# Normed rows of x on GpSimd, a longer warm-up and other first DMA durations in a planned two-layer kernel

## The chip, the cores and the metric

The kernel runs on one core of one Trainium2 chip. A core has five engines with instruction queues of their own: TensorE (PE, matrix products; its weight loads are shown apart as PEld), VectorE (DVE), ScalarE (ACT), GpSimd (POOL) and SyncE (SP, which here issues every DMA). The metric is device time in microseconds, the median of several runs. Lower is better.

## The reference

The input is x, 2 sequences of 1024 rows with 256 features, a context of 154 rows per sequence, and one condition vector per sequence. Two layers follow each other.

```
# layer 0: cross attention with adaptive layer norm
h   = (x - mean) / sqrt(var + eps)                # per row of x, and of the context
xq  = (1 + scale_q) * h + bias_q                  # scale, bias from silu(cond) @ Wss_q + bss_q
xkv = the same on the context rows, with Wss_kv
q, k, v = xq @ Wq + bq, xkv @ Wkv + bkv           # 16 heads of 16
x   = x + softmax(q k^T / 4) v @ Wp + bp
# layer 1: mixture of three experts
nx  = layernorm(x) * gamma + beta
evidence = softmax((nx Wq1)(ctx Wk1)^T / 16) (ctx Wv1)
combined = [nx, evidence, cond]                   # 768 features
probs = softmax(combined @ router_W + router_b)
h_e = silu(combined @ e_w1[e] + e_b1[e])          # 512 wide, three experts
routed = sum_e probs[e] * (h_e @ e_w2[e] + e_b2[e])
g   = sigmoid(silu(combined @ gate_w1 + gate_b1) @ gate_w2 + gate_b2)
out = x + g * (routed @ out_w + out_b)
```

So each row of x is normed twice, once ahead of each layer: its mean is subtracted and the result multiplied by its reciprocal deviation.

## The kernel before, in words

The 2048 rows of x are 16 tiles of 128 rows. Layer 0 (`layer0`) runs 128 steps, 8 for each tile: scores on PE into PSUM, the row maximum on DVE (`mx`, L929), the exponential on ScalarE (L952), a split in two halves of fp16 (`ehl`, L636 on ScalarE and L643 on DVE), a transposing DMA into `et`, and on PE the product with the values (`vm`). `half_done` and `tile_done` divide by the sum (`rc`, `an`, `ao`, L868 to L870), project and add to x (`xa`, L890). The second sequence's rows are in `xb`.

A second stream (`fill`, and after it `dense`) prepares layer 1's weights (`nx`, `evh`, `evl`, `vs`, `vsr`, `ab`) and then computes layer 1 by blocks of one or two pairs of tiles: first the expert layer (`zh`, `zl` and `wh`, `wl`, `wr` against `nx` and `vsr`), tanh on ScalarE (`th`, L1390), a product on DVE (L1393), a split on POOL (`hh` at L638, `hl` at L643), and then the second matrices (`w2oh`, `w2ol`). Numbers are split in a high and a low fp32r part, and three products of parts replace one fp32 product.

The norm of the rows needs four pieces. `stats` computes mean and variance of one tile on DVE (L670, L671). `rstd` turns variances into reciprocal deviations by three Newton steps on tiny tiles (L652 to L665): the first four operations' integer part is on DVE, and the rest is on DVE where `soon` is set, else on POOL. Then one `tensor_scalar` per tile subtracts and multiplies and writes `xn`, a buffer of which two exist: ahead of layer 0 in `front_norm` (L803), ahead of layer 1 in `a` of `front1` (L1021). PE transposes `xn` (L619), and ScalarE applies scale and bias (`full`, L826 and L1028). `moments(i0, i1)` computes the statistics of tiles i0 to i1 ahead of layer 0; its first call also takes the three tiles of context rows (`ctn`) and computes all six deviations together. The context rows are normed on DVE at L1115.

The prologue (`start`) computes scale and bias from the condition vector (`adaptive`, for the context with the weights `wsskv` and for x with `wssq`: 16 small matmuls into PSUM, a copy `ss` on ScalarE, a transpose on PE, and `ada` on DVE), norms and transposes the context, applies scale and bias to it (`xk`, L1124 on ScalarE), and makes keys and values. Meanwhile PE runs `WARM` matmuls on zeros (`warm`), whose results nobody reads, so that it doesn't idle.

The order of all instructions on each engine is not the order of the source. `Plan` builds a graph of all instructions, gives each a duration (`price`), and lists them by rank with a table of durations; `MOVES` is a list of random changes of the ranks that are kept where they shorten the planned total. The resulting order of each engine is then fixed by dependencies (`pin`). A warm-up matmul has the lowest rank: it stands where the plan finds PE without other work. A DMA's planned duration is its bytes divided by a rate. SP issues all DMAs in the planned order: before the change the context rows, the first two tiles of x, `vec` (the small vectors, the condition among them), `wsskv`, `wssq`, the key weights, the query weights, two more tiles of x, the value weights and so on.

Of the kernel before, what the change touches and what calls it, by code (L numbers as in the profile page):

```python
# [16 lines left out]
ALU = mybir.AluOpType  # L17
# [6 lines left out]
NT = 16  # L24
# [3 lines left out]
HK = 160  # L28
EPS = 1e-5
NE = 3  # L30
WARM = 60
RAW = 6
LEAD = 1
BLOCKS = ((0, 1), (1, 1), (2, 2), (4, 2), (6, 2))
NSTEP = 8 * NT
PACE0, PACE1 = 1500.0, 2100.0
MOVES = (1100001, 1100005, 1100019, 1100033, 1100059, 1100068, 1100087, 1100091, 1100170, 1100261, 1100302,
         1100322, 1100329, 1100338, 1100420, 1100424, 1100527, 1100533, 1100618, 1100719, 1100724, 1100868,
         1100955, 1100984, 1100999, 1101051, 1101060, 1101194, 1101201, 1101272, 1101290, 1101335, 1101413,
         1101426, 1101441, 1101487, 1101528, 1101561, 1101574, 1101614, 1101671, 1101704, 1101924, 1102111,  # L40
         1102322, 1102606, 1102710, 1102758, 1102833, 1103118, 1103684, 1104487, 1104919, 1105278, 1105605,
         1105610, 1105611, 1105652, 1105670, 1105798, 1105925, 1106150, 1107392, 1107479, 1107593, 1107732,
         1107777, 1107785)


V_BQ, V_BSSQ, V_BSSKV, V_GAM, V_BET, V_COND, V_BK, V_B2 = 0, 2, 6, 10, 12, 14, 18, 20
# [3 lines left out]
class Later:  # L50


    def __init__(self):
        self.now, self.due = 0, {}
# [50 lines left out]
class Plan:  # L105
# [5 lines left out]
    SBUF = 212800  # L111

    def __init__(self, tc):
        self.tc, self.nc = tc, tc.nc
        self.side, self.tiles, self.names = {}, {}, 0
        self.kept = {}
        self.streams = set()
        self.joint = {}
        self.apart = {}
# [154 lines left out]
    def price(self, node, op):  # L274

        ins, eng = node.ins, node.eng
        aps = [a for a in ins.ins if hasattr(a, "bass_ap")]
        outs = [a for a in ins.outs if hasattr(a, "ap")]
        node.cost = 50.0
        if not outs:  # L280
            return
        n = count(list(outs[0].ap)[1:])
        if eng == "SP":
            b = count(outs[0].ap) * mybir.dt.size(outs[0].dtype)
            turn = "Transpose" in op
            node.cost = b / 311.0 if not turn else b / 160.0
            node.load = 900.0 if not turn and outs[0].dtype == FP16 else 650.0 if turn or (len(outs[0].ap) > 2 and b < 200000) else 475.0
            node.wide = 1470.0 if turn else node.load
            return
        widths = [count(list(a.ap)[1:]) for a in aps]  # L290
        psum = any(self.side.get(self.tiles.get(str(getattr(a.bass_ap.tensor, "name", "")).rpartition("_")[0],
                                                ("",))[0]) == str(PSUM) for a in aps)
        ptr = sum(1 for w in widths[1:] if w == 1 and n > 1)
        wide = [a for a, w in zip(aps, widths) if w > 1 or n == 1]


        flat_ = sum(self.side.get(self.tiles.get(str(getattr(a.bass_ap.tensor, "name", "")).rpartition("_")[0],
                                                 ("",))[0]) != str(PSUM) for a in wide)
        node.port = eng == "Pool" or (eng == "DVE" and op not in ("TensorReduce", "BNStats", "BNStatsAggregate", "Reciprocal")
                                      and not (len(wide) == 1 and psum) and flat_ > (0 if len(wide) == 1 else 1))  # L300
        if eng == "PE":
            m, four = widths[-1], aps[-1].dtype in (F32, F32R)
            passes = 1 if aps[0].dtype != F32 else 2 if ins.is_transpose else 4
            node.cost = max(passes * n / 2.4, 20.0) + 2.5 + (5.9 + 0.0172 * n if aps[0].dtype == F32R else 0.0)
            node.load = (m / 4 if not four else 4 * m if passes == 4 else 2 * m) / 2.4
            node.rows = list(aps[0].ap)[0][1] / P
            if list(outs[0].ap)[0][1] == 32:

                node.cost, node.load = node.cost / 3, node.load / 3
            if ins.name in self.joint:  # L310

                node.rows, node.step, node.cost = 1.0, node.cost, 280.0
        elif eng == "Activation":
            node.cost = 0.833 * n + (50 if psum else 94) + 93 * ptr
        elif eng == "Pool":
            node.cost = (0.83 * n + 36 if op == "Memset" else 2.08 * n + 160 if op == "TensorTensor" else 0.833 * n + 160)
        elif not aps:
            node.cost = 10.0 + 1.04 * n
        else:
            w = max([n] + widths)  # L320
            single = sum(1 for k in widths if k > 1) == 1 and not psum and op != "TensorReduce"
            node.cost = (335.0 if op == "BNStats" else 290.0 if op == "ISA" else 115.0 if op == "Reciprocal" else 75.0 if w < 16
                         else (0.52 if single else 1.04) * w + 65 + 64 * ptr)
# [218 lines left out]
def tile_pixart_cross_moe(  # L542
# [27 lines left out]
    V, S, G, T, Q = nc.vector, nc.scalar, nc.gpsimd, nc.tensor, nc.sync  # L570
# [74 lines left out]
    def rstd(out, var, n, pool, soon=False):  # L645


        E = V if soon else G
        v = tl(pool, [P, n], F32, f"nwv{n}")
        h = tl(pool, [P, n], I32, f"nwh{n}")  # L650
        t = tl(pool, [P, n], F32, f"nwt{n}")
        V.tensor_scalar(v, var, EPS, None, ALU.add)  # L652
        V.tensor_scalar(h, v.bitcast(I32), 1, None, ALU.logical_shift_right)
        V.tensor_scalar(h, h, -1.0, float(0x5F3759DF), ALU.mult, ALU.add)
        E.tensor_scalar(v, v, -0.5, 1.0, ALU.mult, ALU.mult)
        cur = h.bitcast(F32)
        for _ in range(3):
            E.tensor_tensor(t, cur, cur, ALU.mult)
            if soon:
                E.tensor_tensor(t, t, v, ALU.mult)  # L660
                E.scalar_tensor_tensor(out, t, 1.5, cur, ALU.add, ALU.mult)
            else:
                E.tensor_tensor(t, t, v, ALU.mult)
                E.tensor_scalar(t, t, 1.5, 1.0, ALU.add, ALU.mult)
                E.tensor_tensor(out, t, cur, ALU.mult)  # L665
            cur = out

    def stats(mv, src, pool):
        st = tl(pool, [P, 6], F32, "bnst", 2)[: src.shape[0]]
        V.bn_stats(st, src)  # L670
        V.bn_aggr(mv, st)  # L671
# [9 lines left out]
    xres = [xa[:, i] for i in range(NT // 2)]  # L681
    mv0 = tl(per, [P, 20, 2], F32, "mv0")
    rs0 = tl(per, [P, 20], F32, "rs0")
# [36 lines left out]
    CT = (P, P, 52)  # L720
# [65 lines left out]

    def moments(i0, i1):

        k0 = 4 + i0
        if i0 == 0:  # L790
            k0 = 0
            for i, n in enumerate(CT):
                stats(mv0[:n, i], ctn[:n, i], ta)
        for i in range(i0, i1):
            stats(mv0[:, 4 + i], xres[i], l0)
        k = slice(k0, 4 + i1)
        rstd(rs0[:, k], mv0[:, k, 1], 4 + i1 - k0, l0, i0 == 0)

    def front_norm(hb):
        xns = []  # L800
        for i in range(2 * hb, 2 * hb + 2):
            xn = tl(l0, [P, 256], F32, "xn", 2)
            V.tensor_scalar(xn, xres[i], mv0[:, 4 + i, 0:1], rs0[:, 4 + i : 5 + i], ALU.subtract, ALU.mult)  # L803
            xns.append(xn)
        return xns

# [91 lines left out]
    def layer0(later):  # L898
        ao, ets = None, []
        for p in range(NSTEP):  # L900
            ti, j = divmod(p, 8)
            b, q0 = ti // 8, (ti % 2) * P
            if j == 0:
                ao = tl(l0, [P, 256], F32, "ao", 2)
                if ti == 1:
                    moments(4, NT // 2)
                if ti == 6:
                    while len(xres) < NT:
                        yield
                    moments(8, NT)  # L910
                if ti % 2 == 0 and ti + 2 < NT:
                    front(ti // 2 + 1, later)
            if j % 4 == 0:
# [81 lines left out]
    def front1(hb, later):  # L995
# [14 lines left out]
        def a():  # L1010
            if hb == NT // 4:
                ones(1)
            mv = tl(keep["lf"], [P, 2, 2], F32, "mv1", 2)
            rs = tl(keep["lf"], [P, 2], F32, "rs1", 2)
            for i in range(2):
                stats(mv[:, i], xres[t0 + i], keep["lf"])
            rstd(rs, mv[:, :, 1], 2, keep["lf"], hb < 2)
            st["xn"] = []
            for i in range(2):
                xn = tl(l0, [P, 256], F32, "xn", 2)  # L1020
                V.tensor_scalar(xn, xres[t0 + i], mv[:, i, 0:1], rs[:, i : i + 1], ALU.subtract, ALU.mult)  # L1021
                st["xn"].append(xn)

        def t():
# [82 lines left out]

    def start():

        adaptive(1)  # L1110
        adaptive(0)
        moments(0, 2)
        norm, turn, q, stack = front(0, None, first=True)
        for i, n in enumerate(CT):
            V.tensor_scalar(ctn[:n, i], ctn[:n, i], mv0[:n, i, 0:1], rs0[:n, i : i + 1], ALU.subtract, ALU.mult)  # L1115
# [66 lines left out]
        G.tensor_scalar(bph, bpr, 1.0, 1.0, ALU.mult, ALU.mult)  # L1182
        G.tensor_scalar(f(bph), f(bph), mneg, 1.0, ALU.mult, ALU.mult)
        G.tensor_tensor(bp2[0:2], f(bph), bpr, ALU.add)
        moments(2, 4)
        trA.close()


# [399 lines left out]
```

## Time and profile before

| what | value |
|---|---|
| median of 3 runs | 403.0 us (402.08 to 403.06) |
| the profiled execution's own time | 405.18 us |
| its span, first to last instruction | 403.4 us |
| mean granted clock of PE | 0.989 |
| busy, share of the span | PE 96%, PEld 82%, DVE 77%, ACT 56%, POOL 51% |
| DMA | 40.60 MB in packets, 101 GB/s on average |

All durations below come from one profiled execution, which was 2.18 us slower than the median. In the profile, a line such as L615 is often a helper's: all matmuls stand at L615, all transposes at L619, all splits at L636 to L643, and only the names of the tiles tell which is which. Busy time counts overlapping matmuls once. "Granted clock" is the share of full speed at which PE was allowed to run.

### The profile page before, as it was taken

What the parts mean: (1) busy time and instruction counts of PE and PEld (TensorE: products, weight loads), DVE (VectorE), ACT (ScalarE), POOL (GpSimd) and SP (SyncE); (2) the same over time, 40 slices, a digit from 0 to 9 for tenths busy, and PEclk for the clock granted to TensorE, in tenths of its full rate; (3) what the DMA queues carried; (4) which work ended last, traced back from release to release, by engine and by line L of the source; (5) the groups of instructions that cost most, each with busy time, mean ns of one, the idle gap of its engine ahead of it and who ended that gap; (6) DMA issues with size and microseconds to landing.
All of it is one profiled execution on the core that took longest, in us unless ns stands there. A gap on an engine that the chain in (4) does not pass through costs nothing. (4 is left out here: it accounts for less than half of the span.)

```text
span 403.4 us, 8995 instructions
## 1 busy us (share of the span) xinstructions
PE 388.0 (96%) x3206; PEld 331.1 (82%) x3206; DVE 309.3 (77%) x837; ACT 226.2 (56%) x607; POOL 206.4 (51%) x369
## 2 busy tenths in 40 slices
PE   6999999789999999999999999999999999999995
PEld 4787776577799999999879888888788989888884
DVE  7468988989998998989968887889787748323224
ACT  1589898776657756777665655476763042222111
POOL 4584743320156476377248553652656483655361
PEclk9999999989999999999999999999999999999998
DMA  7914657968374436443547443774534000100001
GB/s 224 349 31 149 246 159 177 205 200 187 84 110 85 67 68 123 87 80 67 83 87 144 86 114 72 157 153 107 80 65 68 2 0 2 52 2 0 2 0 52
DMA packets 89547, 40.60 MB, mean 101 GB/s; under 512 B 75684, under 2 KB 84891, under 8 KB 89503
## 3 DMA queue, kind: packets, MB, share of 16 engines
q1 hardware_dynamic: 89503, 40.03, 43.5%
q8 instruction: 25, 0.41, 0.4%
q14 instruction: 19, 0.16, 0.1%
HBM read 16.59 MB, written 5.08 MB: 54 GB/s over the span
## 5 line engine op out<-in xcount | busy, mean ns | idle before, releaser
L952 ACT ACTIVATE S<-S,mx 128x154 f32<-128x154 f32 x224 | 70.3, 386 | 32.6 <-DVE mx L929 32.5
L615 PE MATMUL D<-zh,nx 128*128 128x512 f32 (+1 forms) x280 | 81.7, 362 | 0.0
L1390 ACT ACTIVATE th<-D 128x512 f32<-128x512 f32 (+1 forms) x70 | 37.2, 531 | 74.0 <-PE D L615 40.9
L643 POOL TENSOR_TENSOR hl<-th,hh 128x512 fp32r<-128x512 f32 (+1 forms) x70 | 74.9, 1072 | 6.2 <-PE D L615 1.7
L638 POOL TENSOR_SCALAR hh<-th 128x512 fp32r<-128x512 f32 (+1 forms) x70 | 38.2, 547 | 72.1 <-DVE th L1393 57.2
L1393 DVE SCALAR_TENSOR_TENSOR th<-th,D 128x512 f32<-128x512 f32 (+1 forms) x70 | 40.1, 575 | 30.7 <-ACT th L1390 30.3
L615 PE MATMUL D<-w2oh,hh 128*128 128x256 f32 x192 | 54.5, 287 | 0.8 <-ACT acc L1410 0.8
L615 PE MATMUL D<-w2ol,hh 128*128 128x256 f32 x192 | 54.5, 287 | 0.0
L615 PE MATMUL D<-w2oh,hl 128*128 128x256 f32 x192 | 54.3, 288 | 0.0
L615 PEld LDWEIGHTS D<-zh,nx 128*128 128x128 f32 x280 | 48.4, 189 | 5.7 <-issue 0.5
L929 DVE TENSOR_REDUCE mx<-S 128x4 f32<-128x616 f32 x64 | 49.2, 791 | 3.4 <-PE S L615 2.9
L615 PE MATMUL D<-zl,nx 128*128 128x512 f32 (+1 forms) x140 | 49.8, 357 | 0.0
L643 DVE TENSOR_TENSOR ehl<-S,ehl 128x616 f16<-128x616 f32 x56 | 44.2, 794 | 5.0 <-ACT ehl L636 4.8
L615 PE MATMUL D<-wh,vsr 128*128 128x512 f32 (+1 forms) x140 | 40.1, 357 | 0.0
L636 ACT CAST ehl<-S 128x616 f16<-128x616 f32 x56 | 39.7, 715 | 0.3
L615 PEld LDWEIGHTS D<-w2oh,hh 128*128 128x128 f32 x192 | 36.3, 190 | 1.7 <-POOL hh L638 1.0
L615 PEld LDWEIGHTS D<-w2ol,hh 128*128 128x128 f32 x192 | 36.3, 190 | 1.1 <-issue 0.7
L615 PEld LDWEIGHTS D<-w2oh,hl 128*128 128x128 f32 x192 | 36.1, 190 | 0.8 <-issue 0.4
L1436 DVE SCALAR_TENSOR_TENSOR acc<-D,pr,acc 128x256 f32<-128x256 f32 x48 | 21.3, 478 | 18.5 <-PE D L615 18.3
L615 PEld LDWEIGHTS D<-zl,nx 128*128 128x128 f32 x140 | 26.3, 188 | 3.5 <-issue 0.5
L615 PEld LDWEIGHTS <-et 128*128 128x128 f16 x640 | 22.5, 96 | 7.2 <-issue 5.3
L615 PEld LDWEIGHTS D<-wh,vsr 128*128 128x128 f32 x140 | 24.8, 188 | 4.1 <-issue 0.6
(245 smaller groups left out, 867.6 us busy)
## 6 DMA issues: line engine op xcount, KB each, us to landing
raw<-in_w_dram SPq DMA_DIRECT2D x9, 512.0 KB, 4.4
wd<-vs SPq DMA_DIRECT2D x3, 768.0 KB
vsr<-wd SPq DMA_DIRECT2D x3, 768.0 KB, 5.9
out_dram<-th SPq DMA_DIRECT2D x16, 128.0 KB, 1.7
raw<-in_w2T_dram SPq DMA_DIRECT2D x3, 512.0 KB, 5.5
raw<-in_gw_dram SPq DMA_DIRECT2D x4, 256.0 KB, 3.0
xb<-in_x_dram SPq DMA_DIRECT2D x2, 512.0 KB, 4.9
et<-ehl SPq DMA_TRANSPOSE x56, 3.6
```

The source lines that it names most:

```text
L615: return T.matmul(out, lhsT, rhs, start=start, stop=stop, skip_group_check=not group)
L636: return S.copy(hi, src)
L638: return G.tensor_scalar(hi, src, 1.0, 1.0, ALU.mult, ALU.mult)
L643: return round_(he, hi, src), le.tensor_tensor(lo, src, f(hi) if hi.dtype == F32R else hi, ALU.subtract)
L929: top = V.tensor_reduce(mx, ps[:, :, 0 : 2 * LK].rearrange("p u (i k) -> p u i k", i=2), AX.X, ALU.max, negate=True)
L952: e = S.activation(e, e, AF.Exp, bias=mx[:, n // 2, n % 2 : n % 2 + 1]).ins
L1390: S.activation(th, ps, AF.Tanh, scale=0.5)
L1393: V.scalar_tensor_tensor(th, th, 1.0, ps, ALU.add, ALU.mult)
L1436: V.scalar_tensor_tensor(acc[:, t], po[:, k], pr[:, t, s : s + 1], acc[:, t], ALU.mult, ALU.add)
```

## The change

- The normed rows `xn` are computed on POOL instead of DVE, in `front1` for all tiles and in `front_norm` for all but the first pair.
- `moments` counts the context's three tiles as 0 to 2 and the tiles of x from 4. The prologue calls it for the context alone, ahead of the first `adaptive`, and then for the first two tiles of x, between the two. The deviations of the context and of these two tiles of x so come from two chains of `rstd` instead of one, both on DVE.
- In `price`, a DMA's planned duration is multiplied by 1.37 and is at least 450 ns for the first 1.6 MB that are loaded.
- `WARM` is 80 instead of 60, and `MOVES` has other entries (37 instead of 68), so every engine's order is drawn up anew.

```diff
-WARM = 60
+WARM = 80
...
-MOVES = (1100001, 1100005, 1100019, 1100033, 1100059, 1100068, 1100087, 1100091, 1100170, 1100261, 1100302,
...
+MOVES = (1100018, 1100033, 1100062, 1100087, 1100158, 1100174, 1100261, 1100393, 1100417, 1100510, 1100511,
...
     def __init__(self, tc):
+        self.came = 0.0
...
             node.cost = b / 311.0 if not turn else b / 160.0
+            if self.came < 1.6e6:
+
+                node.cost = max(1.37 * node.cost, 450.0)
+            self.came += b
...
     def moments(i0, i1):

-        k0 = 4 + i0
-        if i0 == 0:
-            k0 = 0
-            for i, n in enumerate(CT):
-                stats(mv0[:n, i], ctn[:n, i], ta)
         for i in range(i0, i1):
-            stats(mv0[:, 4 + i], xres[i], l0)
-        k = slice(k0, 4 + i1)
-        rstd(rs0[:, k], mv0[:, k, 1], 4 + i1 - k0, l0, i0 == 0)
+            if i < 3:
+                stats(mv0[: CT[i], i], ctn[: CT[i], i], ta)
+            else:
+                stats(mv0[:, i], xres[i - 4], l0)
+        rstd(rs0[:, i0:i1], mv0[:, i0:i1, 1], i1 - i0, l0, i1 < 7)

     def front_norm(hb):
...
-            V.tensor_scalar(xn, xres[i], mv0[:, 4 + i, 0:1], rs0[:, 4 + i : 5 + i], ALU.subtract, ALU.mult)
+            (V if hb == 0 else G).tensor_scalar(xn, xres[i], mv0[:, 4 + i, 0:1], rs0[:, 4 + i : 5 + i], ALU.subtract, ALU.mult)
...
                 if ti == 1:
-                    moments(4, NT // 2)
+                    moments(8, 12)
...
-                    moments(8, NT)
+                    moments(12, 4 + NT)
...
                 xn = tl(l0, [P, 256], F32, "xn", 2)
-                V.tensor_scalar(xn, xres[t0 + i], mv[:, i, 0:1], rs[:, i : i + 1], ALU.subtract, ALU.mult)
+                G.tensor_scalar(xn, xres[t0 + i], mv[:, i, 0:1], rs[:, i : i + 1], ALU.subtract, ALU.mult)
...
     def start():

+        moments(0, 3)
         adaptive(1)
+        moments(4, 6)
         adaptive(0)
-        moments(0, 2)
...
-        moments(2, 4)
+        moments(6, 8)
         trA.close()
```

## The prediction

> **What bounds the kernel now.** I read the page first: busy shares, then the span in 40 slices.
>
> ```profile
> span 403.4 us, 8995 instructions
> PE 388.0 (96%) x3206; PEld 331.1 (82%) x3206; DVE 309.3 (77%) x837; ACT 226.2 (56%) x607; POOL 206.4 (51%) x369
> PE   6999999789999999999999999999999999999995
> DVE  7468988989998998989968887889787748323224
> POOL 4584743320156476377248553652656483655361
> PEclk9999999989999999999999999999999999999998
> ```
>
> TensorE (PE) is the bound: it is short of full only in the first slice, in slices 8 and 9, and at the end. VectorE (DVE) comes second, near 90% for the first two thirds; GpSimd (POOL) is half idle. So what counts is where PE stands still. The table by stretch (length, then busy time of PE, PEld, DVE, ACT, POOL, granted clock) says where:
>
> ```profile
> 60.00:100.00 40.00, 35.08 (x300) 26.78 (x295) 36.80 (x106) 29.90 (x79) 10.27 (x15) 0.96 0.80 190
> 100.00:140.00 40.00, 39.85 (x366) 34.89 (x365) 36.80 (x112) 26.34 (x76) 18.54 (x37) 1.00 0.50 93
> 140.00:180.00 40.00, 40.00 (x421) 37.49 (x420) 36.74 (x101) 26.96 (x79) 24.06 (x51) 1.00 0.47 90
> ```
>
> Only between 60 and 100 us does PE lose much, 4.92 us, with DVE busy 92% and POOL 26%. From 100 us on, PE has no room. The same table over five shorter stretches shows the clock:
>
> ```profile
> 5.18:8.60 3.42, 1.14 (x22) 0.84 (x21) 3.04 (x22) 0.21 (x1) 0.40 (x2) 1.00 1.01 297
> 8.60:12.01 3.41, 3.41 (x38) 1.88 (x28) 1.53 (x7) 0.35 (x2) 0.00 (x0) 0.50 1.07 364
> 12.01:15.42 3.41, 3.41 (x32) 2.98 (x31) 2.43 (x11) 2.01 (x6) 1.14 (x4) 1.00 1.06 349
> 76.87:80.28 3.41, 2.12 (x28) 1.40 (x28) 3.35 (x10) 2.32 (x5) 1.65 (x3) 1.00 1.23 154
> 80.28:83.69 3.41, 3.41 (x17) 3.18 (x14) 3.07 (x7) 2.13 (x6) 2.90 (x8) 0.50 0.97 294
> ```
>
> Twice PE runs a slice of 3.41 us at half clock, each time just after a slice that it left part idle. A pause is therefore paid twice. The prologue, from the timeline of PE (start, duration, what, idle before):
>
> ```profile
> 8.23 0.79 PE L615 MATMUL S<-raw,csil 128*32 128x128 f32 x16 [2.28 <-DVE nwt L658]
> 8.96 1.68 PE L615 MATMUL D<-warm 128*128 128x256 bf16 x7
> 10.42 0.42 PE L619 MATMUL S<-ident,ss 128*128 128x128 f32 x1
> 10.78 1.08 PE L615 MATMUL T<-raw,csil 128*32 128x128 f32 x16
> 11.79 1.03 PE L615 MATMUL D<-warm 128*128 128x256 bf16 x7
> ```
>
> And the waits of PE between 60 and 100 us, longest first, with the rows for the operation that moves:
>
> ```profile
> PE T L619 <- DVE xn L1021: 1.9, 1, 1.9
> ```
> ```profile
> L1021 DVE TENSOR_SCALAR xn<-xa,mv,rs 128x256 f32<-128x256 f32 x8 | 3.8, 500 | 0.0
> L803 DVE TENSOR_SCALAR xn<-xb,mv,rs 128x256 f32<-128x256 f32 x8 | 4.7, 608 | 0.0
> L638 POOL TENSOR_SCALAR hh<-th 128x256 fp32r<-128x256 f32 x28 | 11.8, 424 | 25.6 <-DVE th L1393 22.4 <-PE S L615 1.4 <-PE D L615 0.9
> ```
>
> The one long stall of PE is a wait for normed rows.
>
> **The change, part by part.** *Warm-up.* WARM goes from 60 to 80. In the new order 40 stand ahead of the first real matmul (before: 25), then 7, 8, 7 and 11 (before 7, 7, 1 and 13); one group of 7 past 25 us is in both. Before, 25 took 4.90 us from 1.05, PE then idled 2.28 us, and the clock dropped at 8.60. The first real matmul waits for its 512 KB transfer (its last part landed at 8.10); the four transfers ahead of it only change their order among themselves, so 8.23 stays. Now 15 more warm-ups, at 0.11 us each at full clock, fill 1.6 us of the pause. With the clock kept, the steps from 8.23 cost: 16 adaptive matmuls 0.58 (what the same shape takes at L615 at 27.49), 7 warm-ups 0.76, transpose 0.11, 8 warm-ups 0.87, 16 matmuls 0.58, 7 warm-ups 0.76, transpose 0.11, the first three context transposes 0.33 and 0.22 to the start of ScalarE. That is 4.32 us; before, ScalarE began xk at 13.59, 5.36 us after 8.23. I take **-1.0**. Ends: -1.7 (all that a 3.41 us slice at half clock can cost) and +0.7 (all 40 at the cold 196 ns: 1.05 + 7.84 = 8.9 instead of 8.23).
>
> The Trainium skill, page "TensorE: Matmul & The Clock Gate", Part 1, says that the gate's window is free-running, about 3.4 us, with a phase that differs from run to run. The slices above have that length; by the page's rule the gain would be between nothing and the whole 1.7 in single runs.
>
> *Context's deviations by themselves.* One chain of 12 small DVE operations on six columns becomes two of 12 on three and two, that is 12 more. Before, the chain ran 6.11 to 8.56 with a step each 0.20, and independent ones 0.08 apart (6.51, 6.59). The two chains interleave in the new order, so **0**. The cover: context rows were normed by 11.68 at the latest, only because an `ada` step stood ahead of two of them, and PE now asks for them near 12.0. If nothing interleaves it is 12 x 0.20 = 2.4, rows ready at 12.1 and some 0.3 late: ends 0 and +0.3. vec's transfer goes first, the context's 0.5 later each; that lies in the same cover.
>
> *Order's table.* The longer durations reach the program only through the order. SP keeps all transfers; rbc, the last rows of x and bpr move up, wk from place 18 to 20. wk was issued at 12.52 and its first matmul ran at 41.17: **0**; a place costs 0.37 to 1.3 us of SP there, so it stays covered.
>
> *Rows normed on POOL.* All but the first two of 32: 14 of L803, 16 of L1021. DVE loses 8.1 + 7.0 = 15.1 us; no row shows this operation on POOL, so I take the nearest, L638 of the same size, 0.42 us, 12.7 us in all: POOL goes to 219 of 403. Ends for one: 0.36 (as on DVE undisturbed, 363 ns) and 0.74 (POOL's two-input row of that size). What is on PE's path is the stall at 76.2. There the chain of L652 to L661 ran from 72.70 to 77.10, with two subtractions of ehl (0.80 each), one of vsr (0.68) among it and one of vs (0.68) plus rc (0.2) behind. In the new order one ehl, vs and rc come after the chain, and one ao (0.36) joins: 1.68 - 0.36 = 1.3 us sooner, less some 0.2 to hand over to POOL. So -1.1 of the 1.93, and even chances that the half-clock slice after it (worth 1.7) goes: -0.85. I take **-2.0**. Ends: -6.6 (the whole 4.92 and 1.7) and +1.9 (the stall as long again).
>
> From 100 us on, 22 rows move. Nothing is gained on DVE, since PE is full: **0**. The cover is POOL's idle time, over 40% there; a pair holds POOL 0.85, and `hh`/`hl` of the dense part queue behind it. Without cover 11 x 0.85 = +9.4; I keep +3 (a third) and -1 as ends, nearer to 0, because POOL's own waits there are for its inputs (22.4 of 25.6 us on L1393).
>
> The Trainium skill, page "GPSIMD Engine Reference", section 4.1, advises against this: elementwise work belongs on VectorE, GpSimd being about twice as slow with two inputs, though roughly level with one. This trace agrees on one input (424 against 500 ns). At twice the price the 30 rows would take 12 us more of POOL, still beside PE but for the stall's first row, +0.4.
>
> *New order.* PE runs the same 2919 matmuls besides warm-ups. Their order is drawn anew (37 moves instead of 68). Turns between transposes and fp32r matmuls fall from 90 to 75, all turns between kinds from 335 to 329. A 512-column step after a transpose takes 0.31 (30.81 to 31.12) against 0.24: 6 x 0.08 = **-0.5**; ends -1.2 (15 turns) and +2 (a new stall as long as the measured one).
>
> Sum: -1.0 - 2.0 - 0.5 = -3.5 us. The profiled execution took 405.18 (span 403.4 and 1.78 around it), 2.18 over the median; it would take 401.7, and the median 403.0 goes to **399.5**.
>
> **Rivals.** *Hidden anyway.* Between 60 and 100 us DVE is at 92%, so PE may merely wait for the next thing there, a vs or ehl subtraction, and give the prologue's us back. For it: the short waits on vs (0.6), xa (0.5) and ex (0.5). Against: 4 of the rows, 2.71 us, leave DVE in just this stretch. It leaves -0.5: 402.5.
>
> *POOL late (slower).* In the new POOL order a pair waits for its deviations and for the two xn buffers, which PE's transposes free, while evl, zh/zl or hh/hl stand behind. For it: one pair of normed rows stands right behind another there, ahead of evl. If three of the 15 pairs stall PE by the measured 1.9 and one brings a half-clock slice, 3 x 1.9 + 1.7 = 7.4, net +3.9: 406.9. It decides from 0.31 us a pair on (3.5 + 1.2 over 15 pairs). Against: 10.27 us of POOL in 40.
>
> *The stretch heals.* All 6.6 go: -1.0 - 6.6 - 0.5 = -8.1: 394.9. Against: DVE stays near 85% there.
>
> **How the numbers follow.** A measurement of this kernel tells 0.3% (1.2 us) from no change. Forecast 0.52 (397 to 401.5, all faster), hidden 0.18 (401.5 to 403.5, some 0.04 of it faster, the rest same), POOL late 0.23 (403.5 to 408; 0.02 of it within 0.3%), healed 0.07. Faster 0.52 + 0.07 + 0.04 = 0.63; same 0.14 + 0.02 = 0.16; slower 0.21. The range leaves out a tenth on either side: half of the healed case with some of the forecast's edge below 396.0, and half of POOL late above 405.0. The forecast's own range is 397 to 401.5.
>
> **What would show it.** Right: PE idle between its first warm-ups and 8.2 shrinks from 2.28 to under 1, no half-clock slice near 10 us, xk on ScalarE at about 12.5; PE busy over 37 of 40 in 60 to 100; the wait for xn under 1 us; DVE near 295, POOL near 219. Wrong: a wait of PE on xn from POOL in several places, new idle of PE after 100 us with hh or hl named, a POOL row of xn well over 0.42, or a clock slice at half speed elsewhere.

## The result, and the profile after

The changed kernel took 422.69 us (median of 5, 422.16 to 424.42) against 403.06 of the kernel before (median of 5 on the same chip, 402.08 to 404.86): a ratio of 1.0472 [1.0439, 1.0505]. I had forecast 399.5 and a range up to 405.0. The forecast was wrong by sign and by 23 us. The profiled execution took 422.16, with a span of 420.3, 16.9 over the span of the profiled execution before.

The page of the changed kernel, busy shares and slices:

```profile
span 420.3 us, 9047 instructions
PE 397.8 (95%) x3226; PEld 335.3 (80%) x3226; DVE 297.2 (71%) x820; ACT 226.7 (54%) x607; POOL 241.8 (58%) x399
PE   9999998799999999998899999999998999999995
POOL 4594854611087469459348951853676586474361
PEclk9999999769999999999999999999999999999999
```

DVE fell to 297.2, as expected (295). POOL rose to 241.8 where I had expected 219: 30 more instructions brought 35.4 us, 1.18 each, not 0.42. The answer about the tile `xn` (duration of one: least, median, most, in ns) says it outright:

```profile
L1020 POOL TENSOR_SCALAR xn<-xa,mv,rs x8: 1218/1225/1328, 76.6 to 192.4; 128x256 f32<-128x256 f32 x8
L802 POOL TENSOR_SCALAR xn<-xb,mv,rs x8: 1223/1226/1234, 131.6 to 236.5; 128x256 f32<-128x256 f32 x8
L802 DVE TENSOR_SCALAR xn<-xa,mv,rs x2: 405/408/412, 10.5 to 10.9; 128x256 f32<-128x256 f32 x2
```

A row costs POOL 1.22 us, three times what it costs DVE, and a pair of rows 2.44. The waits of PE over the whole execution (us in total, times, longest) show who pays:

```profile
PE T L621 <- POOL xn L1020: 6.1, 7, 1.9
PE D L617 <- POOL hh L640: 1.3, 2, 1.1
PE T L621 <- POOL xn L802: 0.8, 2, 0.4
```

Where one wait for `xn` stood before, there are nine, almost all on L1020, the rows ahead of layer 1. The table by stretch (length, then busy PE, PEld, DVE, ACT, POOL, clock):

```profile
60.00:100.00 40.00, 34.85 (x273) 26.42 (x271) 31.88 (x92) 27.86 (x76) 14.86 (x19) 0.83 0.74 172
100.00:140.00 40.00, 38.26 (x345) 32.76 (x344) 34.80 (x110) 26.43 (x72) 20.43 (x38) 1.00 0.52 102
140.00:180.00 40.00, 39.03 (x390) 36.50 (x388) 32.65 (x88) 25.47 (x75) 27.24 (x49) 1.00 0.57 80
...
100.00:300.00 200.00, 192.41 (x1722) 166.52 (x1721) 161.19 (x430) 122.35 (x338) 117.06 (x198) 1.00 0.52 94
```

From 100 to 300 us PE was idle for 0.6 us before and is idle for 7.6 now. PE had no room there, and now has gaps in every stretch. From 60 to 100 us it is as busy as before (34.85 against 35.08), but its clock is 0.83 instead of 0.96, since four slices in a row run at half speed:

```profile
75.10:78.51 3.41, 1.17 (x22) 0.86 (x22) 3.19 (x11) 3.25 (x7) 1.88 (x2) 1.00 0.83 245
78.51:81.93 3.42, 2.80 (x24) 1.72 (x26) 1.57 (x3) 1.02 (x2) 3.42 (x4) 0.50 1.21 224
81.93:85.34 3.41, 3.13 (x13) 2.41 (x13) 1.55 (x4) 2.21 (x7) 3.23 (x6) 0.50 0.45 187
85.34:88.75 3.41, 2.92 (x28) 2.76 (x28) 3.30 (x15) 2.61 (x9) 0.62 (x5) 0.50 0.39 82
88.75:92.17 3.42, 3.42 (x17) 2.84 (x15) 2.32 (x11) 0.37 (x1) 0.00 (x0) 0.50 0.81 202
```

Before, one slice ran so here. Three more cost up to 3 x 1.7 = 5.1 us. With the 7.0 of new idle time from 100 to 300, 1.4 from 300 to 340 and 0.9 from 340 to 380, these places hold up to 14.4 of the 16.9 us. The prologue went the other way: ScalarE began `xk` 0.8 us sooner (12.82 instead of 13.59). So some 3 us I could not place.

The beginning of it, on POOL and on PE:

```profile
76.64 2.44 POOL L1020 TENSOR_SCALAR xn<-xa,mv,rs 128x256 f32<-128x256 f32 x2 [4.69 <-DVE rs L663]
79.05 2.43 POOL L802 TENSOR_SCALAR xn<-xa,mv,rs 128x256 f32<-128x256 f32 x2
```
```profile
77.91 0.44 PE L621 MATMUL T<-ident,xn 128*128 128x128 f32 x2 [1.90 <-POOL xn L1020]
79.13 0.69 PE L621 MATMUL T<-ident,xn 128*128 128x128 f32 x2 [0.78 <-DVE vs L645]
```

Before, the same pair and the transposes that read it stood in the timeline like this:

```profile
77.74 0.69 DVE L1021 TENSOR_SCALAR xn<-xa,mv,rs 128x256 f32<-128x256 f32 x2
78.16 0.76 PE L619 MATMUL T<-ident,xn 128*128 128x128 f32 x4 [1.92 <-DVE xn L1021]
```

The pair began 1.10 us sooner (76.64 instead of 77.74), just as the forecast had it. But then POOL needed 1.22 for the first row and 1.22 for the second, where DVE had both done in 0.69, and PE stood for 1.90 us, as long as before, and for 0.78 once more. The second of these waits is put down to `vs`, but the second row, which ended at 79.08, is what PE's transposes at 79.13 read.

### The profile page after: what moved, and what is told of

Read it like the earlier page. It is cut to its first block, busy times and chain, and to the rows that moved or that the text cites. A ratio compares the mean times of both kernels' runs of the same rounds, so it can differ in the third digit from the quotient of the medians.

```text
span 420.3 us, 9047 instructions
## 1 busy us (share of the span) xinstructions
PE 397.8 (95%) x3226; PEld 335.3 (80%) x3226; DVE 297.2 (71%) x820; ACT 226.7 (54%) x607; POOL 241.8 (58%) x399
## 5 line engine op out<-in xcount | busy, mean ns | idle before, releaser
L617 PE MATMUL D<-zh,nx 128*128 128x512 f32 (+1 forms) x280 | 79.9, 361 | 0.0
L617 PE MATMUL D<-w2oh,hh 128*128 128x256 f32 x192 | 55.5, 292 | 1.7 <-ACT acc L1410 0.8
L638 ACT CAST ehl<-S 128x616 f16<-128x616 f32 x56 | 39.2, 707 | 1.0 <-DMA et<-ehl 0.5
```

The lines of the kernel that those rows point to most:

```text
L617: return T.matmul(out, lhsT, rhs, start=start, stop=stop, skip_group_check=not group)
L638: return S.copy(hi, src)
```

## The experiments

Two theories stood against each other. *Price:* the whole loss comes from a row's 1.22 us on POOL, on the way from a tile's statistics to PE. *Order:* the loss is the new order's, whatever a row costs, since PE had hardly any room and every change of the order risks some. A third was that POOL's queue as such is too full, so that `hh` and `hl` come late. All ratios below are to the kernel before, run on the same chip in the same round; a ratio need not be the quotient of the two medians.

**One part at a time, in fixed orders.** To keep an order while moving an operation to another engine, the plan is told that the instruction still belongs to the old engine, and the planned start gives its place on the new one. PE, ScalarE and SP then have exactly the order of the kernel that is taken as a base; on DVE and POOL only the 30 rows differ.

```diff
-                node, me = Node(ins, str(ins.engine).split(".")[1]), len(nodes)
+                node, me = Node(ins, self.other.get(ins.name, str(ins.engine).split(".")[1])), len(nodes)
...
-                V.tensor_scalar(xn, xres[t0 + i], mv[:, i, 0:1], rs[:, i : i + 1], ALU.subtract, ALU.mult)
+                o = G.tensor_scalar(xn, xres[t0 + i], mv[:, i, 0:1], rs[:, i : i + 1], ALU.subtract, ALU.mult)
+                plan.other[o.ins.name] = "DVE"
```

The change's order, all rows on DVE:

> The order of every engine is that of the changed kernel, instruction by instruction; only the 30 normed rows run on DVE, in the places that the plan gave them on POOL. Theory 1 (the operation itself is slow on POOL: 1.22 us against 0.4 to 0.6 on DVE): nearly all of the 19.6 us goes, 400 to 405 us. Theory 2 (the new order, with its moves, warm-ups and DMA durations, is at fault): it stays at 417 to 423 us, since the order is the same.

Measured: 411.64 us, 1.0196 [1.0133, 1.0260].

The order before, all 30 rows on POOL:

> The order of every engine is that of the kernel before; only the 30 normed rows run on POOL, at the planned times they had on DVE. Theory 1: the eight pairs ahead of layer 1 each hold PE by about 1.6 us more (2.44 for a pair on POOL against 0.8), 13 us, and the half-clock slices after that come on top: 415 to 425 us. Theory 2: the order is the old one, so 402 to 406 us.

Measured: 414.59 us, 1.0256 [1.0199, 1.0313].

The order before, only the 16 rows ahead of layer 1 on POOL:

> The order of the kernel before, only the 16 rows ahead of layer 1 (L1021) on POOL. Theory 1: these are the rows that PE waits for (6.1 of its 6.9 us of waiting for normed rows in the changed kernel), so four fifths of what all 30 cost: 412 to 420 us. If instead POOL's occupation is what costs (35 us more busy time, hh and hl behind it), the price goes with the number of rows, 16 of 30: about half, 410 to 412 us. Theory 2: 402 to 406 us.

Measured: 413.82 us, 1.0237 [1.0180, 1.0293].

The order before, only the 14 rows ahead of layer 0 on POOL:

> The order of the kernel before, only the 14 rows ahead of layer 0 (L803, without the first pair) on POOL. Theory 1: their deviations are known long before, so little: 402 to 406 us. If POOL's occupation is what costs, 14 of 30 of the price: 409 to 412 us. Theory 2: 402 to 406 us.

Measured: 405.23 us, 1.0020 [0.9990, 1.0051].

So without any of the other parts of the change, moving the rows costs 10 us, and of these the eight pairs ahead of layer 1 cost 9. The 14 rows ahead of layer 0 put 17 us more on POOL and cost nothing that can be told. That speaks against the third theory: what hurts is the delay of the pairs ahead of layer 1, and not POOL's occupation. PE's waits with all rows and with layer 1's alone:

```profile
PE T L625 <- POOL xn L1029: 7.9, 9, 2.3
PE T L625 <- POOL xn L809: 1.5, 2, 1.0
```
```profile
PE T L625 <- POOL xn L1027: 8.1, 10, 2.3
```

The first of the four shows little by itself. Its 411.64 us lie between what the two theories had named, and an order drawn for rows on POOL may put them at places that are poor for DVE, so it can bear both causes.

**What a row's price is made of.** Seven operations on a tile of ones, five of them at 128 x 256 and one each at 128 and 512 columns, stand in the prologue of the kernel before, where POOL has room. Their durations are read from the timeline alone.

```diff
+    form("pp256", 256, fc[:, 0:1], fc[:, 1:2], ALU.subtract, ALU.mult)
+    form("pp128", 128, fc[:, 0:1], fc[:, 1:2], ALU.subtract, ALU.mult)
...
+    form("ppma", 256, fc[:, 0:1], fc[:, 1:2], ALU.mult, ALU.add)
+    form("pimm", 256, fc[:, 0:1], 1.0, ALU.mult, ALU.mult)
...
+    form("isub", 256, 0.5, 0.5, ALU.subtract, ALU.mult)
```

> The kernel before with seven extra one-input operations on POOL in its prologue, on a tile of ones whose results nobody reads: two column scalars with subtract and mult at 128, 256 and 512 columns (the form of the normed rows), two column scalars with mult and add, one column scalar with a constant (mult and mult, subtract and mult), and two constants with subtract and mult. If the two column scalars are what is slow: 1.22 us at 256 columns with either pair of operations, 0.42 with constants, something between with one; about 0.7 at 128 and 2.3 at 512 if the price goes with the columns. If the subtraction is slow: 1.22 also with constants and subtract, 0.42 with mult and add.

```profile
6.49 1.07 POOL L753 TENSOR_SCALAR isub<-fs 128x256 f32<-128x256 f32 x1
...
11.63 0.56 POOL L753 TENSOR_SCALAR ppma<-fs,fc 128x256 f32<-128x256 f32 x1
12.17 0.48 POOL L753 TENSOR_SCALAR pimm<-fs,fc 128x256 f32<-128x256 f32 x1
12.62 1.14 POOL L753 TENSOR_SCALAR psub<-fs,fc 128x256 f32<-128x256 f32 x1
```

It isn't the scalars that come from columns: with two constants a subtraction and a product take 1.07 (`isub`), and a product and an addition with two columns take 0.56 (`ppma`). A later run read the order of the two operations and the subtraction alone:

```diff
+    form("iam", 256, 0.5, 0.5, ALU.add, ALU.mult)
+    form("ims", 256, 0.5, 0.5, ALU.mult, ALU.subtract)
+    form("isa", 256, 0.5, 0.5, ALU.subtract, ALU.add)
+    form("iss", 256, 0.5, None, ALU.subtract, None)
+    form("pam", 256, fc[:, 0:1], fc[:, 1:2], ALU.add, ALU.mult)
+    form("pms", 256, fc[:, 0:1], fc[:, 1:2], ALU.mult, ALU.subtract)
```

> The kernel before with six more operations on GpSimd in the prologue, 128 x 256 each, on ones, read from the trace alone: add then mult, mult then subtract, subtract then add, and subtract alone with constants; add then mult, and mult then subtract with column scalars. If any subtraction is slow: the three with constants near 1.07, the one with columns near 1.2. If only subtract ahead of mult is: near 0.5 for all. If add ahead of mult is slow too: 1.07 for it, and then it is the order of the two operations.

```profile
6.48 0.41 POOL L753 TENSOR_SCALAR iam<-fs 128x256 f32<-128x256 f32 x1
6.85 1.07 POOL L753 TENSOR_SCALAR ims<-fs 128x256 f32<-128x256 f32 x1
7.89 1.08 POOL L753 TENSOR_SCALAR isa<-fs 128x256 f32<-128x256 f32 x1
8.94 0.86 POOL L753 TENSOR_SCALAR iss<-fs 128x256 f32<-128x256 f32 x1
9.79 0.55 POOL L753 TENSOR_SCALAR pam<-fs,fc 128x256 f32<-128x256 f32 x1
10.33 1.30 POOL L753 TENSOR_SCALAR pms<-fs,fc 128x256 f32<-128x256 f32 x1
```

An addition ahead of a product takes 0.41 (`iam`), 0.55 with columns (`pam`). With a subtraction in either place it takes 1.07 to 1.08 (`ims`, `isa`), 1.30 with columns (`pms`), and a subtraction alone still 0.86 (`iss`). So this form is slow on POOL where it subtracts, wherever that stands. Once the negative of the mean is at hand, adding it gives the norm in the form of `pam`, in less than half the time.

**The price varied in a fixed order.** With the change's order kept, rows of half the width (only half of the features are normed, and the transposes read that half twice; the rows ahead of layer 0 are changed likewise):

```diff
-                G.tensor_scalar(xn, xres[t0 + i], mv[:, i, 0:1], rs[:, i : i + 1], ALU.subtract, ALU.mult)
+                G.tensor_scalar(xn[:, 0:P], xres[t0 + i][:, 0:P], mv[:, i, 0:1], rs[:, i : i + 1], ALU.subtract, ALU.mult)
```

> The changed kernel in its own order, but each normed row on POOL is written for half its columns and transposed twice (the other half of the features is left out; PE does the same number of matmuls), so that a row costs about 0.65 us instead of 1.22. Theory 1, the price on POOL decides and the order is sound at the price it was drawn for (0.37): most of the loss goes, 405 to 410 us. Theory 3, the order costs some 8 us of itself whatever a row costs: 413 to 417 us (half of the engine's 11 us back).

Measured: 411.68 us, 1.0194 [1.0153, 1.0235]; a row took 0.80.

With the change's order kept, rows of whole width in the quick form (x times the mean plus the reciprocal deviation, so the norm itself is left out; the expectation names the two columns the other way round; the rows ahead of layer 0 likewise):

```diff
-                G.tensor_scalar(xn, xres[t0 + i], mv[:, i, 0:1], rs[:, i : i + 1], ALU.subtract, ALU.mult)
+                G.tensor_scalar(xn, xres[t0 + i], mv[:, i, 0:1], rs[:, i : i + 1], ALU.mult, ALU.add)
```

> The changed kernel in its own order, the normed rows on POOL, but by mult and add (x times the deviation's reciprocal plus the mean, which leaves out the right offset), the form that took 0.56 us instead of 1.22. Nothing else moves. Theory 1 (the row's price): with 0.56 the rows cost what the plan thought, within 0.2 us, and the loss is that of the order alone or none: 402 to 406 us if the order is sound at its own prices. Theory 3 (the order costs some 8 us of itself): 409 to 412 us, as with the rows on DVE.

Measured: 407.51 us, 1.0105 [1.0053, 1.0157]; a row took 0.554.

The same edit in the order before:

> The order of the kernel before, the 30 rows on POOL at the times they had on DVE, but by mult and add (the offset is again not the right one), 0.56 us a row. Theory 1: the 10 us that the move costs in this order came from 1.22 us a row; at 0.56 a pair reaches PE 0.3 to 0.5 us later than from DVE, and DVE is freed: 401 to 406 us. If it is the hand-over between engines that costs, and not the row: 410 us or more.

Measured: 404.21 us, 1.0015 [0.9986, 1.0044]; a row took 0.555.

| a row on POOL | the order before | the change's order |
|---|---|---|
| 1.22 us | 1.0256 [1.0199, 1.0313] | 1.0472 [1.0439, 1.0505] |
| 0.80 us | not run | 1.0194 [1.0153, 1.0235] |
| 0.55 us | 1.0015 [0.9986, 1.0044] | 1.0105 [1.0053, 1.0157] |

With nothing but the price of the row changed, all of the loss that can be told goes in the order before, and some 15 of 19.6 us (422.7 to 407.5, in two rounds) in the change's. There both times, at 0.80 and at 0.55 us a row, lie between what the price theory and the order theory had named: both have a share. The waits for `xn` go with it, in the order before and in the change's:

```profile
PE T L625 <- POOL xn L1029: 1.6, 1, 1.6
```
```profile
PE T L621 <- POOL xn L1020: 1.2, 1, 1.2
```

One wait is left in each, the first pair's, and PE is busy for 199.40 of the 200 us from 100 to 300 in the order before and for 199.01 in the change's. The price theory holds for the 15, the order theory for the last 1% or so (1.0053 to 1.0157).

**The warm-ups alone.** In the order before, 15 more warm-ups ahead of the first real matmul, so that 40 stand there; nothing else differs on any engine.

```diff
+            if "PE" in str(row[0].engine):
+                row[25:25] = self.extra
...
-    for n in range(WARM):
-        mm(ps[:, 0:256], warm[:, 0:P], warm, True, True)
+    for n in range(WARM + 15):
+        one = mm(ps[:, 0:256], warm[:, 0:P], warm, True, True).ins
+        plan.extra += [one] if 25 <= n < 40 else []
```

> The kernel before in its own order, with 15 more warm-up matmuls on PE behind the first 25 (40 ahead of the first real one, as in the changed kernel). By the prediction's first step PE keeps its clock between 8.6 and 12.0 us, and all that follows comes 0.7 to 1.7 us sooner: 402 to 403.5 where the kernel before takes 404.6, its profile without a half-clock slice near 10 us. If the prologue hangs on its transfers: no difference; if the extra matmuls run at half clock: up to 0.7 us slower.

Measured: 404.99 us, 1.0023 [0.9995, 1.0050]. The prologue did what I had predicted. ScalarE begins `xk` at 12.51 instead of 13.59, and the slice near 10 us keeps its clock:

```profile
13.59 0.48 ACT L1124 ACTIVATE xk<-T,ada 128x154 f32<-128x154 f32 x1 [1.40 <-PE T L619]
```
```profile
12.51 0.48 ACT L1130 ACTIVATE xk<-T,ada 128x154 f32<-128x154 f32 x1 [1.31 <-PE T L624]
```

The tables by stretch of the kernel before and of this one:

```profile
8.60:12.00 3.40, 3.40 (x38) 1.87 (x28) 1.52 (x6) 0.34 (x2) 0.00 (x0) 0.50 1.07 364
...
78.40:81.80 3.40, 3.40 (x33) 2.49 (x32) 3.34 (x6) 2.14 (x7) 2.95 (x4) 0.78 0.98 215
81.80:85.20 3.40, 3.40 (x23) 3.40 (x21) 3.06 (x8) 1.78 (x6) 1.47 (x7) 0.72 0.51 199
```
```profile
8.60:12.00 3.40, 3.34 (x51) 2.67 (x52) 2.20 (x10) 0.53 (x2) 0.00 (x0) 1.00 1.08 362
...
78.40:81.80 3.40, 3.40 (x26) 2.26 (x21) 3.33 (x5) 1.74 (x6) 2.86 (x7) 0.50 0.92 290
81.80:85.20 3.40, 3.40 (x19) 3.40 (x19) 2.11 (x5) 1.11 (x4) 0.40 (x4) 0.58 0.44 161
```

The slice at half speed near 10 us is gone, and after the pause at 76 us the time at half speed, which the clocks of these stretches add up to, is about two slices instead of one. A second slice can cost 1.7 us, more than the 1.1 won in the prologue. That is one execution of each kernel; in the median of ten nothing is left of the 1.1, and why is not shown.

**New orders.** The next kernels draw the order anew. First the change with the rows back on DVE and the change's list of moves:

```diff
-            (V if hb == 0 else G).tensor_scalar(xn, xres[i],
+            V.tensor_scalar(xn, xres[i],
...
-                G.tensor_scalar(xn, xres[t0 + i],
+                V.tensor_scalar(xn, xres[t0 + i],
```

> The changed kernel with the normed rows on DVE, and the order drawn anew for that (same moves, warm-ups and DMA durations as the changed kernel). If the 8 us that its order still costs with the rows on DVE come from rows put where DVE has no room, the plan now knows better: 401 to 406 us. If warm-ups, DMA durations or the separate deviations cost them: 409 to 413 us again.

Measured: 409.22 us, 1.0142 [1.0094, 1.0190]. Then the change with the true price of a row in the plan's table and the same moves:

```diff
-            node.cost = (0.83 * n + 36 if op == "Memset"
+            node.cost = (4.8 * n if ptr == 2 else 0.83 * n + 36 if op == "Memset"
```

> The changed kernel, rows on POOL, but the plan is told what such a row takes (4.8 ns a column, 1.23 us instead of 0.37) and draws the order anew. If the wrong price in the plan is the cause: most of the loss goes, 405 to 411 us. If the longer way to PE is the cause whatever the order: 414 to 421 us.

Measured: 418.53 us, 1.0342 [1.0294, 1.0390]. A plan that knows the price wins back 4 of 19.6 us. In the list of waits PE then no longer waits for `xn`, but for other things (`ehl` nine times, 4.6 us in all): this plan moved the loss about, and no plan makes a row quicker. A list of moves searched for rows at 1.22 us was not run, so how much of their price a better order could hide is open.

A list of moves fits one graph only. So moves were searched anew with the kernel's own planner, equally long for each, with the rows in a quick and exact form and its true price in the table:

```diff
+        G.tensor_scalar(nb, mean, -1.0, 1.0, ALU.mult, ALU.mult)
+        G.tensor_tensor(nb, nb, rs, ALU.mult)
...
+                G.tensor_scalar(xn, xres[t0 + i], rs[:, i : i + 1], nb[:, i : i + 1], ALU.mult, ALU.add)
```

All other parts of the change, with this:

> All other parts of the change are kept (warm-ups, the context's deviations by themselves, the longer DMA durations); the rows stay on POOL but as one multiplication and one addition of column scalars (reciprocal deviation, and minus mean times it), planned at 0.56 us, and the list of moves was searched anew for these durations. Theory 'the order was not fitted to the true price': the last per cent goes too, 402 to 405.5 us, level with the run beside it that has none of the other parts. Theory 'another part of the change costs it': 3 us or more above that run, near 407.5. Both expect rows of 0.55 to 0.56 us.

Measured: 406.72 us, 1.0054 [1.0030, 1.0078]. None of the other parts, with this:

> The kernel before with only the rows on POOL, in the same multiply-and-add form, planned at 0.56 us, moves searched anew for as long. Theory 'not fitted': 402 to 405 us, as before, since PE has no room after 100 us; a gain of up to 2 us if the stall at 76 shortens. Theory 'another part costs it': the same 402 to 405, with the run that has those parts 3 us above it.

Measured: 404.21 us, 1.0003 [0.9975, 1.0032]. The change with its rows on DVE, searched:

> The changed kernel with the rows back on DVE and a list of moves searched for that (before the search 409.2 us). Theory 'not fitted': 402 to 406 us, some 4 us below the unsearched one. Theory 'another part costs it': 406 to 409, no better than the unsearched one by more than 2 us.

Measured: 406.26 us, 1.0031 [1.0005, 1.0057]. Once the row has a fair price and the moves are searched, which engine computes it can't be told from the time. Between the first two, half a per cent is left. Three runs were to say whose it is. Without the longer DMA durations:

```diff
-            if self.came < 1.6e6:
-                node.cost = max(1.37 * node.cost, 450.0)
-            self.came += b
```

> As the run with all other parts and a searched order, without the longer DMA durations in the table, searched as long. Theory 'the table costs the half per cent': 403 to 405 us, level with the kernel before. Theory 'it is what is left of a search' and theory 'the context's deviations': 406 to 407.5, as with the table.

Measured: 406.15 us, 1.0033 [0.9999, 1.0067]. With the context's deviations computed as before the change, where the call for the first two tiles takes the context's three columns too:

```diff
-        moments(0, 3)
         adaptive(1)
-        moments(4, 6)
         adaptive(0)
+        moments(4, 6)
```

> As the run with all other parts and a searched order, but with the context's deviations computed together with those of the first two tiles after both adaptive steps, as before the change; searched as long. Theory 'the context's deviations': 403 to 405 us. The other two: 406 to 407.5.

Measured: 402.92 us, 0.9967 [0.9937, 0.9996]. And the very kernel of 406.72 us with moves from other random seeds:

> The same kernel as the one with all other parts and a searched order, the moves searched from other random seeds. Theory 'it is what is left of a search': 1 us or more away from 406.7, to either side. The theories that name a part: 406 to 407.5 again.

Measured: 410.89 us, 1.0167 [1.0118, 1.0216]. The last one settles how far the others can be read: one source, two searched lists, and 4.2 us between them (in two rounds, 1.0054 against 1.0167). PE's stretches from 100 to 180 in that kernel, and in the one of 402.92:

```profile
100.00:140.00 40.00, 39.26 (x370) 34.16 (x370) 37.32 (x115) 28.24 (x80) 19.57 (x43) 1.00 0.56 102
140.00:180.00 40.00, 38.58 (x400) 36.25 (x399) 33.81 (x92) 25.84 (x75) 23.91 (x51) 1.00 0.48 82
```
```profile
100.00:140.00 40.00, 40.00 (x383) 35.86 (x383) 35.96 (x110) 28.47 (x81) 21.26 (x46) 1.00 0.43 67
140.00:180.00 40.00, 40.00 (x405) 37.35 (x405) 33.18 (x91) 26.52 (x78) 26.90 (x62) 1.00 0.47 90
```

No wait for `xn` is in question here; PE just has, or has not, work at hand. So the last 1% of the change's loss is of the size by which orders of the same kernel differ, and it stays open whether the table or the context's deviations have a share in it. The kernel of 402.92 us lies below the kernel before, but it is the best of several draws, and its interval ends at 0.9996.

## Why the prediction was wrong

- **The price of a row, wrong, and this is the step that failed.** I took 0.42 us from the nearest row (`hh`, L638, the same size) with 0.36 and 0.74 as ends; it took 1.22, outside both. The row that I took multiplies by two constants; the moved operation subtracts and multiplies by columns. The size agreed and the operations did not. The columns cost little (0.55 against 0.41), the subtraction the rest (1.07 against 0.41). The trace of before shows no subtraction in this form on POOL, so the price could not be read there. My upper end came from another kind of instruction of that size, which does not bound it; nothing in the trace did, and the range should have said so.
- **The Trainium skill's rule, weighed wrongly.** Of the page "GPSIMD Engine Reference", section 4.1 (elementwise work belongs on VectorE, GpSimd being roughly level with one input), I wrote that the trace agreed on one input. It agreed for a product by constants. Of this operation the runs show 1.22 us on POOL against 0.41 on DVE, so "level" does not hold for it, and for this form the advice was right. At twice the price I had counted +0.4 us. At 0.80 us a row, near that, the change's order took 1.0194 against 1.0105 at 0.55, that is 3.6 us for 0.25 us a row.
- **The stall at 76 us, -2.0: right up to the row's start, wrong in its sum.** The pair began 1.10 us sooner (76.64 instead of 77.74), which is the -1.1 of the sum. With a row at 0.55 that shortens the wait, to 1.2 from 1.9. At 1.22 the first row takes it back: the wait is 1.90 again, 0.78 comes on top for the second row, and the half-clock slices behind became four, not none. My price hid that PE stands there until the first of the two rows is done, so that the row's own length is a part of the stall.
- **22 rows past 100 us, 0 with an end of +3: wrong.** I named POOL's idle time as the cover, but idle time is no cover for a chain. From statistics to deviations, row and transpose, every link waits for the one before, and PE has its transposes of a pair at a fixed place in its order. A pair is 2.44 us on POOL and was planned at 0.75 (0.833 x 256 + 160 ns each, by `price`). The price without cover that I gave, 9.4, is near what layer 1's pairs cost in the order before (9.1), but by luck: it counted eleven pairs at 0.85, and the 9.1 come from eight pairs at 2.44. I dropped two thirds of it, because POOL mostly waited for its inputs. The experiment with layer 0's rows finds no cost of POOL's load (1.0020 [0.9990, 1.0051]), and the one with layer 1's shows that this was not the question.
- **The rival *POOL late* came nearest.** It named PE's wait for a pair from POOL, but laid it to POOL's queue and the two buffers instead of the row's own length, and put it at three stalls and 3.9 us net; seven on L1020 and two on L802 came, with three half-clock slices instead of the one that I gave it. Its chance of 0.23 was too low, as it decides from 0.31 us a pair and the pair's price was the least known number of all. *Hidden anyway* and *The stretch heals* did not come.
- **Warm-up, -1.0: right in the prologue, wrong in the time.** In the changed kernel too the slice near 10 us keeps its clock and the next steps come sooner (`xk` at 12.82 instead of 13.59). Alone, the warm-ups brought 1.0023 [0.9995, 1.0050]. I counted a slice at full speed as won for good; in the one execution profiled the next pause cost about two slices instead of one, and what decides that is not shown.
- **New order, -0.5 with +2 as its end: too small an end.** The change's order at a row's price of 0.55 is 1.0105, that is 4.2 us over the order before (3.1 by the medians), and two lists of moves for one source lie 4.2 apart. Counting turns between kinds of matmul says nothing of this.
- **Context's deviations and the table, 0:** not refuted and not shown. The runs that left out one of them lie on both sides of the kernel before (1.0033 and 0.9967), but two orders of one kernel lie further apart (1.0054 and 1.0167).

## What to carry to other kernels

Before an operation is moved to another engine, take its price from a row with the same operations, not only with the same size; where the trace has none, measure the form in a corner of the kernel, as here. On GpSimd write the subtraction of a tensor-scalar operation as the addition of the negative (0.55 against 1.22 us for 128 x 256 with columns). And ask of a moved operation how long the chain becomes that ends at the bound engine; the free time of its new engine answers another question.

## What the runs showed of the hardware

- A tensor-scalar operation on POOL with a subtraction in either place took 1.07 us at 128 x 256 with constants, with an addition and a product 0.41. Scalars from columns added 0.14 to 0.23 (0.55 against 0.41, 1.22 against 1.07, 1.30 against 1.07).
- Runs of one and the same kernel before took 401.6 us at a mean clock of 1.000 and 405.9 at 0.988 on the same chip: how much of the time PE runs at half speed differs from run to run, and by more than most changes here bring. That agrees with the Trainium skill, page "TensorE: Matmul & The Clock Gate", Part 1, which has the gate's window run freely, with a phase that differs from run to run.
- Slices at half speed can follow each other. Four in a row (13.7 us) followed one pause in the changed kernel, while PE was busy for 2.80 to 3.42 us of each. Whether that pause alone kept the clock down is not shown.
